# Two graph layers on one core: slot gathers restricted to the chunks that can fill them

## The chip, the cores and the metric

The kernel runs on one core of a Trainium2 chip. The metric is the device time of one launch in microseconds (us). Engines are named as in the profile: PE is TensorE, PEld its weight loads, DVE is VectorE, ACT is ScalarE, POOL is GpSimd, SP is SyncE, which issues DMAs.

## The reference, cut to what matters

Input are 16 graphs of 1024 nodes with 64 channels each, a symmetric 0/1 adjacency of some 1.5%, and a node mask of ones. Layer 0 thins each node's neighbours, adds the node itself, and takes three quantiles of every channel over the neighbours that stay. Layer 1 is three graph convolutions and a linear layer.

```python
h = relu(layernorm(x))
rem = neigh & (sk > 1) & (rank % sk == sk - 1) & mask[:, :, None]
rem = rem | swapaxes(rem, 1, 2)
nd = where(rem, 0.0, adj_) > 0                    # live edges, the node itself included
s = sort(where(nd[..., None], h[:, None], inf), axis=2)
nv = nd.sum(2)                                    # live degree of each node
for tau, w in ((0.25, 0.25), (0.5, 0.5), (0.75, 0.25)):
    pos = tau * (nv - 1)
    agg += w * interpolation of s between floor(pos) and ceil(pos)
x = x + mlp(h + agg)
# layer 1: h = relu(layernorm(x)); three times relu(adj @ (h W)) with a fixed scaling,
# the three results side by side through Wl; x = x + relu(...)
```

## The kernel before

Graphs are worked on in eight pairs, one graph on the lower 64 partitions, one on the upper 64. For each pair there are three kinds of work.

**Preparation** (`prepare`, `prepare_one`, L538 to L782). The adjacency is loaded in eight pieces of 128 rows (L616), made into bytes `edge` (L617) and transposed into `edgeT` (L624, L627). L634 clears the diagonal of both with one multiplication each on DVE. Counts and ranks of neighbours come from matmuls with matrices of ones (`sums`, L664, L669); L690 and its neighbours add up edge, removal and transposed removal in `q`, and L695 leaves the live edges in `edge`, with the live degree `nv`. The nodes of a graph are then put in order of their live degree: `place` (L716) is each node's position, L721 (POOL, indirect DMAs) writes the rows of live edges to DRAM by position, L737 reads them back in order, L747 and L750 transpose them into `liveT`. Its rows are the neighbours in eight chunks of 128, its columns the nodes in order of degree. `nvs` (L760) holds the degrees in that order for both graphs, and `number_slots` (L763, L770 to L776) makes `r`: for each neighbour of a node, the running number of its edge.

**Gather** (L874 to L911). Nodes in order of degree are cut into seven blocks and a tail; `BLOCKS` gives first node, end, least and greatest degree. Slot k of a node is its k-th live neighbour. For every slot DVE fills `s` (L888): a comparison of `r` with the slot's number, over all eight chunks of both graphs. PE multiplies `s` with the channels `hp`, split into three bf16 parts: for each chunk, part and graph one matmul of 64 output rows (L895) adds to `pg`. Several slots share a matmul, up to 400 columns. A node with fewer neighbours than slots gets a large number in every second missing slot (`none`, L905, L908). ACT copies `pg` to `g` (L911). `s` has two buffers, `pg` three.

**Sort** (`quantiles`, L850). A sorting network runs over the slots of a block as minima and maxima on DVE (L858), then the quantiles are summed (L863, L871), and `store` (L918, L920) transposes and sends them off. The second layer (`later`) reads them back with L1098 and runs through L1006, L1010, L1039, L1055 and L1071. The tail's slots of several pairs are kept and sorted together.

Two other parts matter. `layernorm_relu` (L509) ends in a multiplication (L520) and a maximum with zero (L521). `bounds` (L965) runs once in each pair: 16 one-column operations on `nvs` (L971), a maximum over them (L975) and one into `worst` (L976), so that a degree outside `BLOCKS` is noticed. At the end `worst` and `odd` (inputs other than 0 and 1) raise a flag, and a branch then runs `general`, which computes everything again without assumptions.

The main loop interleaves the preparation of the next pair with gather and sort of this one, in steps. Gather of a block is put ahead of the sort of the block before it. The last pair's gather and sort are interleaved with the second layer of all pairs. Within that, the framework orders the instructions of each engine when the kernel is built, so that their order can shift with the change; each engine then runs its list in order.

Of the kernel before, what the change touches and what calls it, by code (L numbers as in the profile page):

```python
# [9 lines left out]
F32 = mybir.dt.float32  # L10
# [11 lines left out]
P = 128  # L22
# [17 lines left out]

TAILS = {4: (0, 4), 7: (4, 7)}
TAIL = (1008, 1024, 21, 42)

SPLIT = 592

# [339 lines left out]
def graph_layers_kernel(ctx: ExitStack, tc: tile.TileContext, ins, out: bass.AP):  # L385
# [54 lines left out]
    wcol = const.tile([P, len(TAUS)], F32, name="wcol")  # L440
    for q, (_, w) in enumerate(TAUS):
        nc.vector.memset(wcol[:, q : q + 1], w)
    worst = const.tile([P, 1], F32, name="worst")
    nc.vector.memset(worst, 0.0)

    odd = const.tile([P, NB, NT], F32, name="odd")

# [61 lines left out]
    def layernorm_relu(pool, h, xt, sq, T):  # L509

        stat = pool.tile([P, T], F32, tag="ln_stat", name="ln_stat")
        nc.vector.tensor_reduce(stat, xt, AX.X, ALU.add)
        nc.vector.tensor_scalar(stat, stat, 1.0 / C, None, ALU.mult)
        nc.vector.tensor_tensor(h, xt, stat[:, :, None].to_broadcast([P, T, C]), ALU.subtract)
        nc.scalar.activation(sq, h, AF.Square)
        var = pool.tile([P, T], F32, tag="ln_var", name="ln_var")
        nc.vector.tensor_reduce(var, sq, AX.X, ALU.add)
        nc.scalar.activation(var, var, AF.Sqrt, bias=eps_ln, scale=1.0 / C)
        nc.vector.reciprocal(var, var)
        nc.vector.tensor_tensor(h, h, var[:, :, None].to_broadcast([P, T, C]), ALU.mult)  # L520
        nc.vector.tensor_scalar(h, h, 0.0, None, ALU.max)  # L521

    h_d = [dram.tile([N, C], F32, name=f"h_d{b}") for b in range(NB)]

# [81 lines left out]
    def prepare_one(st, x, pools):  # L606
# [22 lines left out]
                yield  # L629

        nc.sync.dma_start(out=adjT_d[b][:, :, :], in_=edgeT)
        for e in (edgeT, edge):
            own = diagonal(e)
            nc.vector.tensor_tensor(own, own, other_h[:, None, :].to_broadcast([P, NT, P]), ALU.mult, saturate=False)  # L634
        yield
        sums = chunk_sums(edgeT, pools)
        nbp = ps.tile([P, NT], F32, tag="big", bufs=2, name="nbp")
# [41 lines left out]
        for t in range(NT):  # L679
            q = ps.tile([P, N], F32, tag="big", bufs=2, name="q")  # L680
            for hf in range(NH):
                sl = slice(hf * HALF, (hf + 1) * HALF)
                nc.tensor.matmul(out=q[:, sl], lhsT=ident_h, rhs=edge[:, t, sl], start=True, stop=False)
                nc.tensor.matmul(out=q[:, sl], lhsT=ident_16, rhs=stays[:, t, sl], start=False, stop=False)
                if t // 4 == hf:
                    nc.tensor.matmul(
                        out=q[:, t * P : (t + 1) * P], lhsT=ident_h, rhs=ident_h, start=False, stop=False
                    )
                for u in range(4 * hf, 4 * hf + 4):
                    nc.tensor.matmul(  # L690
                        out=q[:, u * P : (u + 1) * P], lhsT=stays[:, u, t * P : (t + 1) * P], rhs=ident_16,
                        start=False, stop=(u % 4 == 3),
                    )

            nc.scalar.activation(  # L695
                edge[:, t, :], q, AF.Relu, bias=bias(-2.0), accum_out=nv[:, t : t + 1], saturate=False
            )
            yield
# [32 lines left out]
        def find_live():  # L731
# [25 lines left out]
            for hf in range(NH):  # L757
                sl = slice(hf * HALF, (hf + 1) * HALF)
                nc.tensor.matmul(out=nv_all[half, sl], lhsT=all_rows, rhs=sums[:, sl], start=True, stop=True)
            nc.scalar.copy(st.nvs[half, :], nv_all[half, :])  # L760
            yield

            def number_slots(side):  # L763
# [110 lines left out]
    def gather(st, block, g, pools):  # L874


        work, ps, _ = pools
        j0, j1, least, slots = block
        W = j1 - j0
        high = missing_high(slots, least)  # L880
        r, at = (st.r[0], j0) if j1 <= SPLIT else (st.r[1], j0 - SPLIT)
        r = r.rearrange("p x u j -> p (x u) j")
        per = max(1, min(HALF // W, 400 // W))
        for k0 in range(0, slots, per):
            n = min(per, slots - k0)
            s = work.tile([P, n, T2, W], BF16, tag="s", bufs=2, name="s")
            for k in range(n):
                nc.vector.tensor_scalar(  # L888
                    s[:, k], r[:, :, at : at + W], float(LIVE + 1 + k0 + k), None, ALU.is_equal
                )  # L890
            pg = ps.tile([P, n, W], F32, tag="pg", bufs=3, name="pg")
            for u in range(NT):
                for part in range(3):
                    for x in range(2):
                        nc.tensor.matmul(  # L895
                            out=pg[x * C : (x + 1) * C], lhsT=st.hp[:, part, x, u, :], rhs=s[:, :, x * NT + u, :],
                            start=(u == 0 and part == 0), stop=(u == NT - 1 and part == 2),
                        )
                if u:
                    continue  # L900
                for k in range(n):
                    if k0 + k + 1 not in high:
                        continue
                    none = work.tile([P, W], BF16, tag="none", bufs=2, name="none")
                    nc.scalar.activation(none, st.nvs[:, j0:j1], AF.Relu, bias=bias(k0 + k + 0.5), scale=-1.0)  # L905
                    for x in range(2):
                        half = slice(x * C, (x + 1) * C)
                        nc.tensor.matmul(  # L908
                            out=pg[half, k], lhsT=ident_big[:, half], rhs=none, start=False, stop=False
                        )  # L910
            nc.scalar.copy(g[:, k0 : k0 + n, :], pg)  # L911

# [39 lines left out]
    def sort_tails(first, end, pools):  # L952
# [8 lines left out]
        quantiles(work, TAIL, (g, t), tail_z[:, :, first:end].rearrange("p q p2 w -> p q (p2 w)"), agg)  # L961
        for p in range(first, end):
            store(p, agg, slice((p - first) * TW, (p - first + 1) * TW), TAIL[0], pools)

    def bounds(st, pools):  # L965

        work = pools[0]
        out_by = work.tile([P, 2 * len(BLOCKS) + 2], F32, tag="out_by", name="out_by")
        for i, (j0, j1, least, most) in enumerate(BLOCKS + (TAIL,)):
            for k, (j, sign, edge) in enumerate(((j0, -1.0, least), (j1 - 1, 1.0, -most))):  # L970
                nc.vector.tensor_scalar(  # L971
                    out_by[:, 2 * i + k : 2 * i + k + 1], st.nvs[:, j : j + 1], sign, float(edge), ALU.mult, ALU.add
                )
        most_by = work.tile([P, 1], F32, tag="most_by", name="most_by")
        nc.vector.tensor_reduce(most_by, out_by, AX.X, ALU.max)  # L975
        nc.vector.tensor_tensor(worst, worst, most_by, ALU.max)  # L976


    def channels_first(pools, src, tag):
# [295 lines left out]
    with ExitStack() as stack:  # L1275
# [7 lines left out]
        with ExitStack() as inner:  # L1283
            early = (
                inner.enter_context(tc.tile_pool(name="early", bufs=1)), keep,
                inner.enter_context(tc.tile_pool(name="ps_early", bufs=1, space=PSUM)),
            )

            ahead = Steps(prepare(0, early))
            ahead.rest()  # L1290
            st = ahead.result
            gather_block(st, 0, pools)
            for p in range(NP - 1):
                ahead = Steps(prepare(p + 1, early))
                for n in range(last + 1):
                    for _ in range(11):
                        ahead.step()
                    if n == 0 and p in TAILS:

                        sort_block(st, n, pools)  # L1300
                        gather_block(st, n + 1, pools)
                        sort_tails(*TAILS[p], pools)
                        continue
                    if n < last:
                        gather_block(st, n + 1, pools)
                    else:
                        ahead.rest()
                        gather_block(ahead.result, 0, pools)
                    sort_block(st, n, pools)
                bounds(st, pools)  # L1310
                st = ahead.result


        with ExitStack() as inner:
# [5 lines left out]
            for n in range(last + 1):  # L1320
# [8 lines left out]
                if n < last:  # L1329
                    gather_block(st, n + 1, pools)  # L1330
                sort_block(st, n, pools)
            bounds(st, pools)
            done.sent = NP
            ahead.rest()

# [1 line left out]
    with ExitStack() as stack:  # L1337
        ps = stack.enter_context(tc.tile_pool(name="ps_flag", bufs=1, space=PSUM))
        most_odd = const.tile([P, 1], F32, name="most_odd")
        nc.vector.tensor_reduce(most_odd, odd.rearrange("p b t -> p (b t)"), AX.X, ALU.max)  # L1340
        nc.vector.tensor_tensor(worst, worst, most_odd, ALU.max)
        pd = ps.tile([1, P], F32, name="pd")
        nc.tensor.transpose(pd, worst, ident)
        most = const.tile([1, 1], F32, name="most")
        nc.vector.tensor_reduce(most, pd, AX.X, ALU.max)
        nc.vector.tensor_scalar(most, most, 0.0, None, ALU.is_gt)
        flag = const.tile([1, 1], I32, name="flag")
        nc.vector.tensor_copy(flag, most)
# [28 lines left out]
```

## Time and profile before

| | |
|---|---|
| median of 3 runs | 3311.39 us (3309.24 to 3313.25) |
| the profiled execution | 3304.46 us, of which span 3302.7 us |
| mean granted PE clock | 0.917 |
| busy: PE / DVE / ACT / POOL | 83% / 81% / 51% / 13% of the span |
| matmuls of gather (L895) | 18432, PE busy with them 1525.3 us |
| fills of `s` (L888) | 1312, DVE busy with them 684.4 us |
| minima and maxima (L858), three largest groups | 319.8, 288.3 and 209.6 us |

An engine's busy time is the union of its instructions' times, so that overlapping instructions are not counted twice. In a group's row stand the operation with its shapes, the count, the busy time, the mean duration in ns, and after the second bar the idle time before its instructions with what ended it.

### The profile page before, as it was taken

What the parts mean: (1) busy time and instruction counts of PE and PEld (TensorE: products, weight loads), DVE (VectorE), ACT (ScalarE), POOL (GpSimd) and SP (SyncE); (2) the same over time, 40 slices, a digit from 0 to 9 for tenths busy, and PEclk for the clock granted to TensorE, in tenths of its full rate; (3) what the DMA queues carried; (4) which work ended last, traced back from release to release, by engine and by line L of the source; (5) the groups of instructions that cost most, each with busy time, mean ns of one, the idle gap of its engine ahead of it and who ended that gap; (6) DMA issues with size and microseconds to landing.
All of it is one profiled execution on the core that took longest, in us unless ns stands there. A gap on an engine that the chain in (4) does not pass through costs nothing. (4 is left out here: it accounts for less than half of the span.)

```text
span 3302.7 us, 69626 instructions
## 1 busy us (share of the span) xinstructions
PE 2727.0 (83%) x29049; PEld 1787.7 (54%) x29049; DVE 2672.2 (81%) x6053; ACT 1691.7 (51%) x3260; POOL 439.7 (13%) x416
## 2 busy tenths in 40 slices
PE   3679978987898789878697898789977689888878
PEld 2446645664566456545464566456644357655545
DVE  4158999899989998898999989898996887874332
ACT  4776547655765566556454765475552323232222
POOL 0211020121012001200101012101103120221110
PEclk9789989998999899989898999799988799989989
DMA  4131113101311130114001310131103110212211
GB/s 132 50 105 59 31 46 105 48 23 37 114 39 34 36 110 33 38 39 119 32 20 42 106 47 23 37 108 45 36 16 69 11 47 11 52 47 59 51 52 40
DMA packets 220069, 177.58 MB, mean 54 GB/s; under 512 B 188001, under 2 KB 188129, under 8 KB 215649
## 3 DMA queue, kind: packets, MB, share of 16 engines
q1 hardware_dynamic: 141824, 125.88, 12.6%
q0 software_dynamic: 16384, 37.77, 3.7%
q10 hardware_dynamic: 61536, 9.39, 1.9%
q8 instruction: 229, 3.75, 0.5%
q14 instruction: 96, 0.78, 0.1%
HBM read 124.44 MB, written 48.55 MB: 52 GB/s over the span
## 5 line engine op out<-in xcount | busy, mean ns | idle before, releaser
L895 PE MATMUL pg<-s,hp 128*64 128x400 bf16 (+5 forms) x18432 | 1525.3, 317 | 92.0 <-DVE s L888 71.9
L895 PEld LDWEIGHTS <-hp 128*64 128x64 bf16 x18432 | 997.6, 112 | 512.5 <-issue 96.6
L888 DVE TENSOR_SCALAR s<-r 128x256 bf16<-128x256 bf16 (+6 forms) x1312 | 684.4, 571 | 122.0 <-PE pg L895 107.9
L911 ACT COPY g<-pg 128x400 f32<-128x400 f32 (+10 forms) x384 | 169.1, 441 | 507.2 <-PE pg L895 445.1
L721 POOL DMA_INDIRECT live_d<-edge,place x128 | 194.3, 1518 | 1061.5 <-DVE place L716 1027.4
L1055 PE MATMUL pg<-adjT,xw 128*64 128x512 fp8e4 x2304 | 294.0, 403 | 44.0 <-issue 22.3
L858 DVE TENSOR_TENSOR t<-g 128x600 f32<-128x600 f32 (+9 forms) x524 | 319.8, 631 | 10.9 <-ACT g L911 9.0
L858 DVE TENSOR_TENSOR g<-t 128x96 f32<-128x96 f32 (+16 forms) x555 | 288.3, 541 | 1.5
L793 ACT ACTIVATE coef<-z,bias 128x200 f32<-128x200 f32 (+6 forms) x480 | 174.3, 402 | 169.1 <-DVE agg L871 153.3
L1055 PEld LDWEIGHTS <-xw 128*64 128x64 bf16 x2304 | 140.7, 115 | 178.9 <-issue 68.4
L1098 POOL DMA_INDIRECT agg<-agg_d,place x128 | 141.9, 1108 | 560.9 <-PE pt L986 312.1
L858 DVE TENSOR_TENSOR t<-t 128x192 f32<-128x192 f32 (+20 forms) x447 | 209.6, 481 | 0.5
L737 POOL DMA_DIRECT2D lp<-live_d x128 | 83.0, 649 | 808.6 <-PE pt L747 772.2
L796 ACT ACTIVATE coef<-coef,wcol 128x200 f32<-128x200 f32 (+7 forms) x512 | 188.9, 399 | 1.8 <-issue 0.7
L619 DVE SCALAR_TENSOR_TENSOR junk_v<-a 128x1024 fp8e4<-128x1024 f32 x128 | 156.4, 1222 | 40.4 <-DMA a<-in_adj 39.2
L750 ACT ACTIVATE liveT<-pt 128x1024 fp8e4<-128x1024 f32 x128 | 129.3, 1024 | 89.7 <-PE pt L747 89.6
L617 ACT ACTIVATE edge<-a 128x1024 fp8e4<-128x1024 f32 x128 | 134.5, 1057 | 62.6 <-DMA a<-in_adj 62.1
L747 PE MATMUL pt<-ident_h,lp 128*128 128x128 bf16 x1024 | 98.8, 254 | 81.0 <-ACT liveT L750 43.5
L713 ACT ACTIVATE junk<-keys,minus 128x1024 fp8e4<-128x1024 f32 x128 | 144.3, 1128 | 38.5 <-PE keys L706 37.4
L776 ACT CAST r<-pr 128x592 bf16<-128x592 f32 (+1 forms) x256 | 141.7, 586 | 42.1 <-PE pr L772 40.9
L695 ACT ACTIVATE edge<-q,bias 128x1024 fp8e4<-128x1024 f32 x128 | 141.9, 1110 | 41.4 <-PE q L690 32.2
L673 ACT ACTIVATE stays<-cs,back 128x1024 f16<-128x1024 f32 x128 | 136.4, 1116 | 35.8 <-DVE look L654 21.4
(172 smaller groups left out, 3768.9 us busy)
## 6 DMA issues: line engine op xcount, KB each, us to landing
a<-in_adj SPq DMA_DIRECT2D x128, 512.0 KB
adjT_d<-edgeT SPq DMA_DIRECT2D x16, 1024.0 KB
lp<-live_d POOLq DMA_DIRECT2D x128, 128.0 KB
adjT<-adjT_d SPq DMA_DIRECT2D x16, 1024.0 KB
room<-in_x SPq DMA_DIRECT2D x16, 256.0 KB
h_d<-room SPq DMA_DIRECT2D x16, 256.0 KB
h_again<-h_d SPq DMA_DIRECT2D x16, 256.0 KB
xt<-in_x SPq DMA_DIRECT2D x16, 256.0 KB
```

Source lines behind the costliest of these rows:

```text
L619: nc.vector.scalar_tensor_tensor(junk, a, 1.0, a, ALU.is_equal, ALU.not_equal, accum_out=odd[:, b, t : t + 1], saturate=False)
L695: nc.scalar.activation(edge[:, t, :], q, AF.Relu, bias=bias(-2.0), accum_out=nv[:, t : t + 1], saturate=False)
L713: nc.scalar.activation(junk, keys, AF.Sign, bias=minus[:, t : t + 1], accum_out=above[:, t : t + 1], saturate=False)
L721: sent = nc.gpsimd.indirect_dma_start(out=live_d[b][:, :], out_offset=bass.IndirectOffsetOnAxis(ap=place[:, b, t : t + 1], axis=0), in_=ed ...
L793: nc.scalar.activation(coef[:, i, :], z[:, at], AF.Abs, bias=bias(rank - (slots + 1) // 2 + tau), scale=sign)
L796: nc.scalar.activation(coef[:, i, :], coef[:, i, :], AF.Relu, bias=wcol[:, q : q + 1], scale=-w)
L858: nc.vector.tensor_tensor(view(bufs, o, n1, n2), view(bufs, a, n1, n2), view(bufs, b, n1, n2), ALU.max if op else ALU.min)
L888: nc.vector.tensor_scalar(s[:, k], r[:, :, at : at + W], float(LIVE + 1 + k0 + k), None, ALU.is_equal)
L895: nc.tensor.matmul(out=pg[x * C : (x + 1) * C], lhsT=st.hp[:, part, x, u, :], rhs=s[:, :, x * NT + u, :], start=(u == 0 and part == 0), st ...
L911: nc.scalar.copy(g[:, k0 : k0 + n, :], pg)
L1055: nc.tensor.matmul(out=pg[cs, :], lhsT=part[:, u, cs], rhs=adjT[x][:, u, sl], start=(u == 0 and k == 0), stop=(u == NT - 1 and k == len(xw ...
L1098: nc.gpsimd.indirect_dma_start(out=agg[:, t, x, :], out_offset=None, in_=agg_d[b][:, :], in_offset=bass.IndirectOffsetOnAxis(ap=place[:, b ...
```

## The change

Neighbours come in ascending order, in eight chunks of 128. Slot k of a node can lie in chunk c only if the node has at most k live neighbours ahead of the chunk and more than k up to its end. A new table `NEAR` gives, for each block: the greatest number of neighbours up to the end of a chunk (`first`), the least number (`end`), and, for high slots, how many nodes at the start of the block are known to have no such slot (`fewer`). Gather takes from it the chunks of every slot and the first column `w0`; fills and matmuls cover these alone. Where no chunk is looked into by all slots of a group, two matmuls with a block of zeros start the sum instead.

The table is checked: for each graph, matmuls of `chunk_to` with `sums` make the number of neighbours up to each chunk, an identity matmul adds `bounds`, and ACT sums what is above zero into `beyond`. This takes the place of the old `bounds` function. The rows of `bounds` are made on POOL at the start, by 97 memsets and 32 small DMAs. Further, the diagonal of `edge` is no longer cleared on DVE: in `q`, the diagonal block is taken from `edgeT` instead. And layernorm's last two operations become one.

```diff
+    bounds = const.tile([C, HALF], BF16, name="bounds")
+    beyond = const.tile([2 * NT, NB], F32, name="beyond")
...
+            for row, pieces in ((c - 1, most), (NT + c - 1, least)):
+                line = setup.tile([1, N], BF16, tag="line", name="line")
+                for value, a, b in pieces:
+                    nc.gpsimd.memset(line[:, a:b], value)
+                for hf in range(NH):
+                    nc.gpsimd.dma_start(
+                        out=bounds[32 * hf + row : 32 * hf + row + 1, :], in_=line[:, hf * HALF : (hf + 1) * HALF]
+                    )
...
-        nc.vector.tensor_tensor(h, h, var[:, :, None].to_broadcast([P, T, C]), ALU.mult)
-        nc.vector.tensor_scalar(h, h, 0.0, None, ALU.max)
+        nc.vector.scalar_tensor_tensor(h, h, 0.0, var[:, :, None].to_broadcast([P, T, C]), ALU.max, ALU.mult)
...
-        for e in (edgeT, edge):
-            own = diagonal(e)
-            nc.vector.tensor_tensor(own, own, other_h[:, None, :].to_broadcast([P, NT, P]), ALU.mult, saturate=False)
+        own = diagonal(edgeT)
+        nc.vector.tensor_tensor(own, own, other_h[:, None, :].to_broadcast([P, NT, P]), ALU.mult, saturate=False)
...
-                nc.tensor.matmul(out=q[:, sl], lhsT=ident_h, rhs=edge[:, t, sl], start=True, stop=False)
+                others = [sl]
                 if t // 4 == hf:
+                    others = [slice(sl.start, own.start), slice(own.stop, sl.stop)]
+                    nc.tensor.matmul(out=q[:, own], lhsT=edgeT[:, t, own], rhs=ident_h, start=False, stop=False)
+                    nc.tensor.matmul(out=q[:, own], lhsT=ident_h, rhs=ident_h, start=False, stop=False)
+                for o in others:
+                    if o.start < o.stop:
+                        nc.tensor.matmul(out=q[:, o], lhsT=ident_h, rhs=edge[:, t, o], start=False, stop=False)
...
+            by = ps.tile([2 * NT, N], F32, tag="big", bufs=2, name="by")
+            for hf in range(NH):
+                sl = slice(hf * HALF, (hf + 1) * HALF)
+                rows = slice(32 * hf, 32 * hf + 2 * NT)
+                nc.tensor.matmul(out=by[:, sl], lhsT=chunk_to, rhs=sums[:, sl], start=True, stop=False)
+                nc.tensor.matmul(
+                    out=by[:, sl], lhsT=ident_h[rows, rows], rhs=bounds[rows, :], start=False, stop=True
+                )
+            junk = work.tile([P, N], F8, tag="junk", name="junk")
+            nc.scalar.activation(
+                junk[: 2 * NT, :], by, AF.Relu, accum_out=beyond[:, b : b + 1], saturate=False
+            )
...
-                    s[:, k], r[:, :, at : at + W], float(LIVE + 1 + k0 + k), None, ALU.is_equal
+                    s[:, k, :, us, w0:], r[:, :, us, at + w0 : at + W], float(LIVE + 1 + k0 + k), None, ALU.is_equal
...
+            looks = [(u, [k for k in range(n) if u in chunks[k]]) for u in range(NT)]
+            looks = sorted((look for look in looks if look[1]), key=lambda look: -len(look[1]))
+            whole = len(looks[0][1]) == n and not w0
+            if not whole:
+                for x in range(2):
+                    nc.tensor.matmul(
+                        out=pg[x * C : (x + 1) * C].rearrange("p k w -> p (k w)"), lhsT=ident_h[C:, :C],
+                        rhs=st.hp[C:].rearrange("p a x t c -> p (a x t c)")[:, : n * W], start=True, stop=False,
+                    )
...
-                            out=pg[x * C : (x + 1) * C], lhsT=st.hp[:, part, x, u, :], rhs=s[:, :, x * NT + u, :],
+                            out=pg[x * C : (x + 1) * C, ks, w0:], lhsT=st.hp[:, part, x, u, :],
+                            rhs=s[:, ks, x, u, w0:], start=(whole and i == 0 and part == 0),
...
-    def bounds(st, pools):
```

Of the chunks of each slot in the block of nodes 592 to 768, for example, the table leaves: slots 0 and 1 chunks 0 to 5, slots 2 and 3 chunks 0 to 6, slots 4 to 12 all eight, slots 13 and 14 chunks 1 to 7, slots 15 and 16 chunks 2 to 7, and slot 16 without the block's first 48 nodes.

## The prediction

> **What bounds the kernel now.** I read the page's busy table and slices first, then the busy time by stage, then the waits of the long middle stage, then the groups of instructions kept apart by shape.
>
> ```profile
> PE 2727.0 (83%) x29049; PEld 1787.7 (54%) x29049; DVE 2672.2 (81%) x6053; ACT 1691.7 (51%) x3260; POOL 439.7 (13%) x416
> ...
> PE   3679978987898789878697898789977689888878
> ...
> DVE  4158999899989998898999989898996887874332
> ...
> PEclk9789989998999899989898999799988799989989
> ```
>
> (The three digit rows are forty equal slices of 82.6 us.) Over the span VectorE and TensorE look alike. By stage they don't:
>
> ```profile
> core 0: us, PE busy (x) PEld busy (x) DVE busy (x) ACT busy (x) POOL busy (x), PEclk, DMA share, GB/s
> 0.00:200.00 200.00, 98.71 (x793) 63.83 (x794) 58.01 (x195) 120.51 (x158) 28.80 (x42) 0.83 0.30 89
> 200.00:2500.00 2300.00, 1959.57 (x22517) 1296.72 (x22516) 2114.43 (x4669) 1360.42 (x2639) 286.72 (x262) 0.93 0.18 56
> 2500.00:2990.00 490.00, 410.96 (x3763) 266.92 (x3763) 394.82 (x1044) 137.49 (x346) 77.71 (x66) 0.87 0.17 33
> 2990.00:3302.70 312.70, 257.74 (x1979) 160.20 (x1977) 104.92 (x148) 73.31 (x118) 46.50 (x48) 0.92 0.19 51
> ```
>
> The first 200 us prepare pair 0 alone; no engine is full. From 200 to 2500 us the pairs overlap: DVE is busy 2114 of 2300 us (92%), PE 85%. From 2500 to 2990 us the last pair is sorted beside the second layer. The last 313 us are the second layer alone, a chain through PE.
>
> ```profile
> PE pt_agg L918 <- DVE agg L871: 93.7, 26, 9.4
> ...
> DVE s L888 <- PE pg L895: 89.4, 48, 5.7
> ...
> PE pg L895 <- DVE s L888: 65.8, 55, 11.1
> ```
>
> These are waits inside 200 to 2500 us: total us, times, longest. PE stands idle for DVE 159 us (first and third line), DVE for PE 89 us. So the middle is set by DVE, with PE close behind; ACT, at 59%, sets nothing.
>
> **What the Trainium skill says.** "VectorE: DVE Perf Modes", section "What auto-detection actually checks": a one-source operation runs in the fourfold mode if its tensors are 16-bit with unit step and the outermost non-unit dimensions are even or equal. The fill of `s` agrees: 221 ns for 256 elements and 989 ns for 3200 give (989-221)/2944 = 0.261 ns per element. "TensorE: Matmul & The Clock Gate", section "Wait, 56ns, not 53.3ns?": back-to-back matmuls start every N/2.4 GHz plus 2.5 ns. In the trace the two column halves start together, and such couples of 352 columns follow each other at 149 ns, couples of 96 at 43 ns: price and width go together, down to the smallest. "TensorEngine Tiling", "Key Properties": a change of tiling mode drains the engine. In the trace a 128x128 matmul of 128 columns is followed after 56 ns by one of its kind and after 149 ns by a 128x64 one, so 93 ns. "GPSIMD Engine Reference", "1. Specifications": POOL shares its SBUF interfaces with VectorE. The copies of L930 take 197 ns at best and 1127 ns in the median, so yes.
>
> **The change, part by part.** First the fills and the matmuls of gather. I ran its two loops over the tables by hand.
>
> ```profile
> L888 DVE TENSOR_SCALAR s<-r 128x3200 bf16<-128x3200 bf16 x208 | 199.4, 989 | 39.8 <-PE pg L895 27.7 <-issue 10.8 <-ACT r L776 1.3
> L888 DVE TENSOR_SCALAR s<-r 128x256 bf16<-128x256 bf16 x336 | 51.3, 221 | 0.0
> L634 DVE TENSOR_TENSOR edge<-edge,other_h 128x1024 fp8e4<-128x1024 fp8e4 x16 | 19.6, 1224 | 20.6 <-PE ptE L624 20.5
> L971 DVE TENSOR_SCALAR out_by<-nvs 128x1 f32<-128x1 f32 x128 | 9.8, 144 | 0.0
> ```
>
> DVE: the 1312 fills stay 1312, but their elements per partition go from 2,099,200 to 1,858,432. The 240,768 fewer at 0.261 ns are **62.8 us**. 824 of the fills become partial; their outermost dimension is the two graphs, which is even, so I take the fourfold mode for all. The clearing of `edge` goes: **19.6 us**. The bounds operations go: 9.8 us, and eight reductions of 170 ns and eight maxima of 160 ns: **12.5 us**. The layernorm's product (1.22 us, L520) and maximum (0.69 us, L521) become one three-operand instruction, priced by the row of L1078 at 1.22 us: 16 x 0.69 = **11.0 us**, half of it in the second layer. Seventeen small memsets and two operations at the end add 1.5 us. DVE sum: 62.8 + 19.6 + 12.5 + 11.0 - 1.5 = **104.4 us less**.
>
> PE: gather's matmuls go from 18,432 to 16,976, and their columns from 6,297,600 to 5,598,592, the new seeding matmuls included. In couples that is 349,504 columns / 2.4 GHz + 728 x 2.5 ns = 147.4 us less. Against it: `by`, four matmuls of 512 columns (216 ns each) for each of 16 graphs, 13.8 us; the 64 seeded groups, whose 64-row operand I take as a mode of its own, two changes of 93 ns, 11.9 us (nothing if it is no change of mode); the split of L683, 192 more matmuls with no more columns, 0.5 us. Sum: **121 us less** at full clock, 132 us at the mean of 0.917.
>
> ACT: 16 activations on `by` at 1.11 us plus 0.19 us for the accumulator (row of L695): 21 us more, spread over 16 graphs, on an engine at 59%. `by` takes one of the two `big` buffers for about 2 us; behind it stand the numbering matmuls (L770). While gather matmuls of the pair before fill PE, that is covered. In pair 0 nothing covers it: 2 x (0.9 to 1.7 + 1.3), so 4 to 6 us, against 2.4 us of clearing, 0.7 us of layernorm and 1.5 us of bounds operations gone there. I book zero for the first 200 us, with ends of -4 and +6.
>
> POOL: 97 memsets and 32 DMA issues before its first scatter (L721), which waits for `place` and starts at 110 us. The small DMAs of L737 take 536 to 650 ns: 32 x 0.65 = 21 us. Memsets: 100 ns for one element and 204 ns for 128 (the rows at the start) make 0.82 ns an element, so 0.94 us for the 16 full lines, 15 us, and some 13 us for the 81 short ones; hand-overs between them add 6 us. That is 55 us. If every busy microsecond of DVE in the first 100 us (39) held POOL up as at L930, 94 us: still ahead of 110. Cost zero; at worst some 20 us at the front. The DMAs are 64-byte pieces on queues with 0.36 of their time in use.
>
> **On the path.** In 200 to 2500 us lie 7/8 of fills, clearing, bounds and prepare's layernorms: 54.9 + 17.2 + 10.9 + 4.8 = 87.8 us, counted in full since DVE sets that stage. From 2500 to 2990 us: 7.9 + 1.6 us and two layernorms, 11 us. In the last chain a few layernorms, 1.5 us. Sum 100 us. PE drops by 6% of its share, DVE by 4%, so DVE's 89 us of waits for `pg` should shrink also; I add 5 us. From the profiled execution's 3304.5 us this makes 3199.5; the median of the runs is 6.9 us above that execution, so **3206 us**, within 3190 to 3222 if this case holds.
>
> **The rivals.**
> - PE sets more than I think: the waits for `pg` and the windows in which PE is 95% busy and DVE 90% (900 to 1000 us) speak for it, the 159 us of PE waiting against it. Then the gain is PE's, 121 to 145 us: about 3175. Chance 0.12.
> - A wait takes the place of half the gain. `s` has two buffers; a fill that is done earlier waits for matmuls that still use the other. Also the order on DVE shifts: most instructions keep their places, but sort and fill are interleaved differently. For it: 48 waits of that kind now. Against it: the matmuls shrink by a larger share than the fills. About 3258. Chance 0.14.
> - Slower: the partial fills lose the fourfold mode. Their 764,800 elements cost 0.26 ns more each in the twofold mode, 199 us, against 104 us saved: 3311 + 95 = 3406; in the onefold mode 3800. It decides as soon as more than half of these elements fall to the twofold mode. Against it: the source of the full fills is strided too and runs fourfold. Chance 0.05.
> - The change doesn't do what it says: a table that is too tight raises the flag, and the general path recomputes all 16 graphs, far beyond any range here. Counted from the inputs, the prefix counts touch the tables and nowhere exceed them. Chance 0.01.
>
> **How the numbers follow.** The forecast has 0.68. The range 3162 to 3262 reaches over the first two rivals and leaves out the last two. About 0.2%, 7 us, is what a measurement here tells from no change. Faster: 0.68 + 0.12 + most of 0.14 = 0.93; within: 0.01; slower: 0.06.
>
> **What would show it.** Right: partial fills lie on the line 154 ns + 0.261 ns per element; DVE busy near 2568 us, PE near 2600; DVE still about 92% busy in the middle; POOL's setup done by 95 us and the first scatter near 110. Wrong: a fill of 2000 elements above 0.8 us; DVE below 90% in the middle with longer waits for `pg`; the first scatter late; a later start of the last stage not explained by these.

## The result and the profile after

The changed kernel takes 3227.23 us (median of 4, 3222.94 to 3232.01) against 3310.31 us (median of 4, 3308.27 to 3313.25): ratio 0.9749, 95% interval 0.9732 to 0.9766, 83 us less. Run again on another chip, its ratio was 0.9792 (0.9778 to 0.9805). The two intervals don't meet, so ratios from different chips are good to about 0.4%, 14 us; where less matters, I compare kernels of one chip. The profiled execution took 3232.01 us, the slowest of its four, with a span of 3230.2 us; so the profiled executions differ by 72 us only.

The busy table and three of its slice rows, of the kernel after:

```profile
PE 2602.9 (81%) x27819; PEld 1728.7 (54%) x27849; DVE 2569.1 (80%) x5895; ACT 1714.2 (53%) x3292; POOL 461.8 (14%) x545
...
PE   3689968987898689867686799689976689898878
...
DVE  4149999899889988998997889988996888793332
...
PEclk9779989998999799988797799889988799899999
```

VectorE (DVE) lost 103.1 us of work, TensorE (PE) 124.1, ScalarE gained 22.5. These are nearly the sums of the forecast (104.4, 121 to 132, 21). What is new is in the eighteenth to twenty-third slice (1370 to 1860 us): PE stands at 6, 7, 6, 8, 6, 7 tenths there, before at 7, 8, 6, 9, 7, 8. By stage, after (columns as in the forecast's table):

```profile
0.00:200.00 200.00, 101.69 (x815) 65.42 (x818) 55.21 (x201) 121.69 (x160) 67.23 (x172) 0.82 0.29 89
200.00:2500.00 2300.00, 1900.59 (x21740) 1271.88 (x21767) 2061.06 (x4554) 1392.93 (x2690) 272.69 (x261) 0.91 0.19 56
2500.00:2990.00 490.00, 405.63 (x3714) 265.55 (x3713) 373.27 (x1030) 144.10 (x353) 91.31 (x80) 0.89 0.17 40
2990.00:3230.20 240.20, 195.02 (x1555) 125.86 (x1554) 79.58 (x111) 55.43 (x90) 30.61 (x32) 0.92 0.18 49
```

DVE is busy 2061 of 2300 us in the middle, 89.6%, where it was 92%, though each window now holds more of the program. The longest waits of DVE and PE in the same stretch, after (total us, times, longest):

```profile
DVE s L962 <- PE pg L993: 135.3, 64, 21.3
...
PE pt_agg L1005 <- DVE agg L933: 91.1, 19, 11.3
...
PE pg L993 <- DVE s L962: 66.3, 33, 11.7
PE pt L796 <- DMA lp<-live_d: 62.7, 18, 22.4
```

The fills' wait for `pg` did not shrink; it rose from 89.4 to 135.3 us, with one wait of 21.3 us. DVE below 90% in the middle with longer waits for `pg` is one of the signs of being wrong that the forecast names. PE has one of 22.4 us, for a DMA.

Fixed windows drift against the program, so I cut both traces at the first fill of each pair. The last pair runs to the last sum of quantiles, the rest follows (lengths in us, profiled executions):

| kernel | start | pairs 0 to 3 | pair 4 | pairs 5, 6 | last pair | rest |
|---|---|---|---|---|---|---|
| before | 202.2 | 312.8, 317.4, 320.1, 320.6 | 362.5 | 321.0, 313.4 | 512.6 | 320.0 |
| after | 205.4 | 304.7, 307.2, 308.7, 309.3 | 381.2 | 311.7, 304.2 | 480.3 | 317.6 |
| difference | +3.2 | -8.1, -10.2, -11.4, -11.3 | **+18.7** | -9.3, -9.2 | **-32.3** | -2.4 |

The six ordinary pairs gained 59.5 us, the last pair 32.3. Pair 4, in which the collected tails are sorted too, lost 18.7.

### What happened in pair 4

POOL in pair 4, after: start, length, instruction, and in brackets the idle time before it. These are the first three of graph 11's eight scatters:

```profile
1684.62 4.10 POOL L770 DMA_INDIRECT live_d<-edge,place  x1 [8.30 <-DVE place L765]
1689.02 14.40 POOL L770 DMA_INDIRECT live_d<-edge,place  x1 [0.30 <-issue]
1703.73 1.22 POOL L770 DMA_INDIRECT live_d<-edge,place  x1 [0.30 <-issue]
```

The same two first scatters in the kernel before:

```profile
1728.71 1.16 POOL L721 DMA_INDIRECT live_d<-edge,place  x1 [7.48 <-DVE place L716]
1730.18 1.03 POOL L721 DMA_INDIRECT live_d<-edge,place  x1 [0.31 <-issue]
```

The second scatter held POOL for 14.40 us instead of about one. PE after, in the same stretch:

```profile
1690.99 1.07 PE L796 MATMUL pt<-ident_h,lp 128*128 128x128 bf16 x16
1714.41 1.89 PE L796 MATMUL pt<-ident_h,lp 128*128 128x128 bf16 x16 [22.35 <-DMA lp<-live_d]
```

In PE's list the transposes of graph 11's rows stood next, their rows were not in DRAM, and the gather matmuls behind them waited too; with them DVE's fills for a free `s`, one of them for 21.3 us. From the first scatter's start to the last one's end the eight took 27.4 us, before 11.2. The kernel before has long scatters elsewhere: the first one of graphs 3, 5, 7, 9 and 13 took 7.62 or 7.63 us each. None of these is left after the change, so that the 128 scatters' total time even fell, from 194.3 to 175.4 us.

### The profile page after: what moved, and what is told of

Read it like the earlier page. It is cut to its first block, busy times and chain, and to the rows that moved or that the text cites. A ratio compares the mean times of both kernels' runs of the same rounds, so it can differ in the third digit from the quotient of the medians.

```text
span 3230.2 us, 67236 instructions
## 1 busy us (share of the span) xinstructions
PE 2602.9 (81%) x27819; PEld 1728.7 (54%) x27849; DVE 2569.1 (80%) x5895; ACT 1714.2 (53%) x3292; POOL 461.8 (14%) x545
## 5 line engine op out<-in xcount | busy, mean ns | idle before, releaser
L993 PE MATMUL pg<-s,hp 128*64 128x400 bf16 (+11 forms) x16848 | 1361.8, 314 | 93.2 <-DVE s L962 92.7
L993 PEld LDWEIGHTS <-hp 128*64 128x64 bf16 x16848 | 907.4, 113 | 452.1 <-issue 75.3
L962 DVE TENSOR_SCALAR s<-r 128x3200 bf16<-128x3200 bf16 (+25 forms) x1312 | 621.1, 520 | 144.2 <-PE pg L993 143.9
L920 DVE TENSOR_TENSOR t<-g 128x600 f32<-128x600 f32 (+9 forms) x524 | 319.8, 628 | 12.9 <-ACT g L998 11.1
L770 POOL DMA_INDIRECT live_d<-edge,place x128 | 175.4, 1371 | 1025.3 <-DVE place L765 870.9
L1129 PE MATMUL pg<-adjT,xw 128*64 128x512 fp8e4 x2304 | 285.5, 400 | 39.6 <-DVE xw L1119 28.9
L920 DVE TENSOR_TENSOR g<-t 128x96 f32<-128x96 f32 (+16 forms) x555 | 285.8, 539 | 1.4
L920 DVE TENSOR_TENSOR t<-t 128x192 f32<-128x192 f32 (+20 forms) x447 | 208.5, 478 | 0.4
L832 PE MATMUL pr<-liveT,upto 128*128 128x512 fp8e4 (+2 forms) x384 | 124.7, 343 | 50.3 <-ACT r L838 41.3
L796 PEld LDWEIGHTS <-lp 128*128 128x128 fp8e4 x1024 | 82.9, 117 | 145.0 <-DMA lp<-live_d 101.0
L762 ACT ACTIVATE junk<-keys,minus 128x1024 fp8e4<-128x1024 f32 x128 | 144.4, 1128 | 29.8 <-PE keys L755 28.7
```

The lines of the kernel that those rows point to most:

```text
L762: nc.scalar.activation(junk, keys, AF.Sign, bias=minus[:, t : t + 1], accum_out=above[:, t : t + 1], saturate=False)
L770: sent = nc.gpsimd.indirect_dma_start(out=live_d[b][:, :], out_offset=bass.IndirectOffsetOnAxis(ap=place[:, b, t : t + 1], axis=0), in_=ed ...
L796: nc.tensor.matmul(out=pt[:, u, :], lhsT=lp[:, u * P : (u + 1) * P], rhs=ident_h, start=True, stop=True)
L920: nc.vector.tensor_tensor(view(bufs, o, n1, n2), view(bufs, a, n1, n2), view(bufs, b, n1, n2), ALU.max if op else ALU.min)
L962: nc.vector.tensor_scalar(s[:, k, :, us, w0:], r[:, :, us, at + w0 : at + W], float(LIVE + 1 + k0 + k), None, ALU.is_equal)
L993: nc.tensor.matmul(out=pg[x * C : (x + 1) * C, ks, w0:], lhsT=st.hp[:, part, x, u, :], rhs=s[:, ks, x, u, w0:], start=(whole and i == 0 an ...
```

## The experiments

Ratios are to the kernel before on the same chip. The first four ran on one chip, the next four on a second, the last four on a third. On the third, the changed kernel took 3249.41 us and the kernel before 3319.29.

| kernel | ratio | 95% interval |
|---|---|---|
| e1_full_fills | 0.9836 | 0.9820 to 0.9852 |
| e2_full_matmuls | 0.9887 | 0.9869 to 0.9905 |
| e3_rest_only | 1.0054 | 1.0037 to 1.0071 |
| e4_short_pause | 0.9719 | 0.9698 to 0.9740 |
| e5_gather_only | 0.9803 | 0.9778 to 0.9828 |
| e6_no_check | 0.9674 | 0.9647 to 0.9701 |
| e7_no_step | 0.9766 | 0.9742 to 0.9791 |
| e8_relief_only | 0.9950 | 0.9931 to 0.9969 |
| e9_after_again | 0.9792 | 0.9778 to 0.9805 |
| e10_double_check | 0.9730 | 0.9712 to 0.9748 |
| e11_one_mode | 0.9678 | 0.9662 to 0.9693 |
| e12_one_mode_pause | 0.9626 | 0.9613 to 0.9640 |

### Which engine sets the gain: fills or matmuls

e1 leaves the fills at all chunks and columns:

```diff
-  s[:, k, :, us, w0:], r[:, :, us, at + w0 : at + W]
+  s[:, k], r[:, :, :, at : at + W]
```

e2 brings the matmuls back to their old number and width in the groups that are not seeded: in place of a chunk that only some slots look into, the matmuls of a chunk that all look into are issued once more, so that the sums are not the right ones. The seeded groups stay narrow:

```diff
+  if whole:
+      most = looks[0]
+      looks = [look if len(look[1]) == n else most for look in looks] + [most] * (NT - len(looks))
```

e3 empties the table, so that both are full, and keeps the rest of the change:

```diff
-  first, end, fewer = NEAR[(BLOCKS + (TAIL,)).index(block)]
+  first, end, fewer = {}, {}, {}
```

e1: 

> The changed kernel, with the fills of s over all chunks and columns as before (DVE busy with them 684 us again, 63 more than in the changed kernel) and the matmuls still restricted. Theory (DVE sets the middle, PE the last stage): seven pairs lose most of 7.85 us each, some 45 us, the last stage little: about 3272 us; with another order around the fifth pair 3250 to 3290. Rival (PE sets the pace throughout): no loss, 3222 to 3235.

e2: 

> The changed kernel, with restricted fills, and with full-width matmuls in all groups that aren't seeded: for a chunk that only some slots look into, the matmuls of a chunk that all look into are issued once more (so the sums, and the output, are not the reference's). PE gets 513,408 columns back, 107 us at full clock; DVE's work is that of the changed kernel. Theory (DVE sets the middle, PE the last stage): the last stage loses about 15 us, the middle up to 20: 3242 to 3262. Rival (PE sets the pace throughout): 3335 to 3350.

e3: 

> The changed kernel with an empty table for gather: fills and matmuls in full, but the diagonal of edge not cleared, the bounds operations gone, layernorm's fused operation, and by with its check in place (POOL's setup too). DVE has 41 us less than before, PE 14 us more, ACT 21 us more. Theory (DVE sets the middle): 3272 to 3290. Rival (PE or ACT sets the pace): 3310 to 3325.

On the same chip e3 takes 3324.33 us, e1 3250.28, e2 3267.83, and e4, which has both restrictions and a pause that is told of below, 3211.60. None of the four has the scatter of 14.40 us (the longest of graph 11 are 7.61, 2.61, 7.11 and 4.16 us), so nothing has to be taken off for the pause. The narrow matmuls alone (e1) bring 74 us, both together (e4) 113; so the narrow fills bring 39 where the matmuls are narrow already. e2 brings 56, but not by its fills alone: its gather matmuls keep PE busy for 1482.9 us, against 1516.8 in e3 and 1361.3 in e4, so that it keeps about a fifth of PE's saving. Whether the two reliefs add up is therefore not shown.

If DVE alone set the middle, e1 would have gained nothing there; its six ordinary pairs take 1867.0 us against 1915.6 in e3. If PE alone set it, e4 would have gained nothing over e1; its six take 1847.6. **Neither engine sets the middle alone.** The expectations for e1 and e2, in which DVE set it, missed: e1 came to 3250 us, not to some 3272, and e2 to 3268, above its 3262.

The last pair is different. It took 506.8 us in e3, 507.7 in e2 with its narrow fills, 481.4 with narrow matmuls alone. There PE sets the time.

Last, e3 is slower than the kernel before, by 18 us, though by the forecast's sums DVE has 41 us less to do (30.6 between the two traces). Its time lies in the range of the rival, but not for the rival's reason, as e8 will show: something in the rest of the change costs more than 18 us.

### What the check costs

e5 is the kernel before with the restricted fills and matmuls alone: no `by`, no rows of `bounds`, the other operations of DVE as before. Its edit is the gather part of the diff above. e6 is the kernel after without the check and its setup on POOL:

```diff
-            by = ps.tile([2 * NT, N], F32, tag="big", bufs=2, name="by")
...
-                junk[: 2 * NT, :], by, AF.Relu, accum_out=beyond[:, b : b + 1], saturate=False
-            )
-            yield
+    nc.vector.memset(beyond, 0.0)
```

e7 is the kernel after without the check's own step, that is, without the `yield` behind `junk`:

```diff
                 junk[: 2 * NT, :], by, AF.Relu, accum_out=beyond[:, b : b + 1], saturate=False
             )
-            yield
```

e8 is e6 with the emptied table of e3.

e5: 

> The kernel before with the restricted gather alone: the table, fills, matmuls and seeds of the changed kernel; both diagonals cleared on DVE, the old bounds operations, layernorm in two operations, and nothing that verifies the table. Against before: DVE 63 us less, PE 135 us less. Theory now (in the middle both engines bind together, each worth about half of what it is relieved of, and the remaining parts of the change gain nothing): 3195 to 3225, no slower than the changed kernel. Rival (DVE sets the middle, as forecast, so that 41 us of DVE's work put back are lost in full): 3255 to 3270.

e6: 

> The changed kernel without the verification of the table (by, bounds, their setup on POOL, and the step of the preparation that by makes); the output stays the reference's. PE has 14 us less than in the changed kernel, ACT 21 us. Theory (the check is on the path by half of its PE time, and its extra step moves the preparation against the gather): 3195 to 3215. Rival (it is covered, as forecast): 3222 to 3232.

e7: 

> The changed kernel with by in place, but without the step of its own that it makes in the preparation (the yield after it is dropped), so that the interleaving of preparation and gather is counted as before. Theory (the moved steps cost, not the operations): 3200 to 3215. Rival (the operations themselves cost, or nothing does): 3222 to 3235.

e8: 

> The kernel before with DVE relieved of 41 us (diagonal of edge, bounds operations, fused layernorm), gather in full, and nothing that verifies a table. PE and ACT have the work of before. Theory (both engines bind together, so that a relief of DVE alone is taken up by PE): 3285 to 3306. Rival (DVE sets the middle, as forecast): 3262 to 3275.

From the medians, against 3324.95 us for the kernel before on this chip: relief of DVE alone 16 us (e8, 3308.82), restricted gather alone 67 (e5, 3257.88), both 106 (e6, 3218.69), both and the check without its step 79 (e7, 3245.91). So the check costs 27 us, where the forecast had zero; and e7's ratio lies between the two of the full change, so the step has no part in it that these runs show: the theory for e7 fell.

e5 fell too, into its rival's range. The same relief of DVE, 41 us by the forecast's sums, brings 16 us beside the full gather (e8) and 39 beside the restricted one (e6 against e5). What a relief of one engine is worth depends on how much the other has to do. Where the 39 us lie is open: in the profiled executions, the fastest of e5 and the slowest of e6, the seven pairs take 2211.6 and 2211.1 us, and e6 is shorter only behind them.

My next theory was that PE's time for the check lies on the path. PE in the changed kernel, at the change into pair 2 (e9, the changed kernel once more):

```profile
801.10 0.38 PE L815 MATMUL by<-sums,chunk_to 128*16 128x512 bf16 x1
801.41 0.38 PE L816 MATMUL by<-bounds,ident_h 16*16 16x512 bf16 x1
801.72 0.38 PE L815 MATMUL by<-sums,chunk_to 128*16 128x512 bf16 x1
802.03 0.38 PE L816 MATMUL by<-bounds,ident_h 16*16 16x512 bf16 x1
```

The four start 0.31 us apart. In e11, told of next, all four have operands of 128 rows, and they start 0.215 us apart:

```profile
763.89 0.38 PE L810 MATMUL by<-sums,chunk_to 128*16 128x512 bf16 x1
764.10 0.38 PE L811 MATMUL by<-bounds,ident_h 128*16 128x512 bf16 x1
```

So each change between operands of 128 and of 16 rows costs some 0.093 us. With as much on entry, an estimate is 1.33 us a graph, 21 us in all, against 13.8 in the forecast. e10 issues the whole block, from `by` to `junk`, a second time behind the first. e11 gives all of `by`'s operands 128 rows, puts `by` ahead of `nv_all`, and has no step for it:

```diff
-    bounds = const.tile([C, HALF], BF16, name="bounds")
+    bounds = const.tile([P, HALF], BF16, name="bounds")
+    nc.vector.memset(bounds, 0.0)
...
-                    out=by[:, sl], lhsT=ident_h[rows, rows], rhs=bounds[rows, :], start=False, stop=True
+                    out=by[:, sl], lhsT=ident_h[:, rows], rhs=bounds, start=False, stop=True
...
-            yield
```

e9: 

> The changed kernel once more, so that the three beside it have it on their chip: about 0.974 of the kernel before. The fifth pair of graphs again some 375 to 382 us, with TensorE standing still behind graph 11's scatters.

e10: 

> The changed kernel with the block that makes the tile by (its four matmuls and the junk reading) issued a second time right behind the first, for every graph; the sum that it leaves in beyond is the same. Theory: the check's TensorE time lies on the path, about 21 us of it for 16 graphs and the wait for junk's reading beside it, so a second copy costs 20 to 30 us: ratio 0.981 to 0.984. Rival, the forecast's own step (the check lies beside other work): no more than 0.3% over the changed kernel, 0.974 to 0.977.

e11: 

> The changed kernel with every matmul of the tile by taking 128-row operands (bounds made 128 rows, zero below and between, and the whole columns of ident_h), with by placed ahead of nv_all, and without by's own step. Theory: the mode changes inside by, about 93 ns for each of four matmuls plus one on entry, 7 to 8 us over 16 graphs, are part of what the check costs, so the ratio falls by 0.2 to 0.4%: 0.970 to 0.972. Rival (they lie beside VectorE's work): the same as the changed kernel within 0.2%.

**The theory fell.** The doubled check puts off the numbering matmuls behind it by another 2.6 us in the first graph of a pair and 1.4 in the second, 31 us in all, and yet e10 is 0.6% faster than e9. Part of this lead is another thing: e10 happens not to have the scatter of 14.40 us. The same scatter in e10:

```profile
1688.86 2.95 POOL L770 DMA_INDIRECT live_d<-edge,place  x1 [0.30 <-issue]
```

Its pair 4 took 366.3 us, that of e9 377.5. But in the six ordinary pairs, too, nothing is lost by the second copy (1838.5 us against 1846.2), and e4, which also is without the long scatter, has a ratio of 0.9719 against 0.9730. e11 keeps the whole check and saves at most 8 us of mode changes; it has the long scatter as e9 has, and yet it is 1.2% (39 us) faster, where 0.2 to 0.4% were expected, and at 0.9678 as fast as the kernel without the check (0.9674, on another chip). What PE, ScalarE and `big` spend on the check is hidden, as forecast; what the check costs comes in another way.

Cutting the traces at the fills shows where. For the seven changes from one pair to the next, in us added up:

| kernel | last fill to the next pair's first | first fill to the thirteenth | sum |
|---|---|---|---|
| before | 123.3 | 277.6 | 400.9 |
| e8 (no check, full gather) | 124.1 | 280.8 | 404.9 |
| e5 (no check) | 112.5 | 275.7 | 388.2 |
| e6 (no check) | 108.5 | 277.6 | 386.1 |
| e11, e12 (by first) | 114.2, 112.1 | 269.9, 268.1 | 384.1, 380.2 |
| after, e9 | 180.9, 177.2 | 231.5, 231.0 | 412.4, 408.2 |
| e10 (twice) | 177.0 | 236.0 | 413.0 |
| e7 (no own step) | 175.8 | 231.8 | 407.6 |
| e3 (full gather) | 181.3 | 241.0 | 422.3 |

There are two kinds and nothing between (e1, e2 and e4 have 173 to 180 us in the first column). With the check behind `nv_all`, some 25 us pass at each change before the next pair's first fill; without it, or with `by` ahead of `nv_all`, 15 to 18. Most of it comes back in the fills after it, and 17 to 33 us over seven changes don't: 21.5 between e7 and e6, 24.0 between e9 and e11. DVE at the change into pair 2, in e9 (start, length, instruction):

```profile
810.36 1.22 DVE L622 TENSOR_TENSOR h_again<-h_again,hp 128x1024 f32<-128x1024 f32 x1
...
813.18 1.22 DVE L624 TENSOR_TENSOR hp<-h_again,hp 128x1024 bf16<-128x1024 f32 x1
...
818.23 0.98 DVE L962 TENSOR_SCALAR s<-r 128x3200 bf16<-128x3200 bf16 x1
```

and in e11:

```profile
803.37 0.98 DVE L961 TENSOR_SCALAR s<-r 128x3200 bf16<-128x3200 bf16 x1
804.28 1.22 DVE L623 TENSOR_TENSOR h_again<-h_again,hp 128x1024 f32<-128x1024 f32 x1
```

In e9 the first fill stands behind the preparation of `hp` and more of the sorting (L920). No wait is marked on it, and what it reads had been there for 8.2 us, as the last copy of the first columns of `r` by ScalarE shows:

```profile
809.37 1.08 ACT L838 CAST r<-pr 128x592 bf16<-128x592 f32 x2
```

At all seven changes of e9 it had been there for 7.4 to 8.3 us, and in e10, where the second check makes it come later, still for 5.4 to 6.7: so the check's own time is swallowed here. The fill simply comes later in DVE's list. Between the last fill and the first stand 89 or 90 DVE instructions in every kernel of the one kind (after, e1 to e4, e7, e9, e10), and 51 or 52 in every kernel of the other. From the operation on `nvs` (L611, at 802.12 us) it is 16.1 us to the fill; in e11 the same operation starts at 796.33, 7.0 us before it. PE over the whole change, from the last fill to the first, e9 and then e11 (busy times in the order of the stage table):

```profile
793.00:818.20 25.20, 18.98 (x149) 10.12 (x147) 24.23 (x98) 20.78 (x47) 2.46 (x3) 0.87 0.17 57
```

```profile
786.20:803.40 17.20, 13.81 (x128) 8.43 (x126) 15.28 (x61) 13.53 (x35) 2.45 (x3) 0.85 0.10 36
```

DVE is busy all through both, but PE idles 6.2 us in the first and 3.4 in the second. Gather's first matmul follows the last fill after 30 us in e9 and 28 in e11 (212.6 and 197.2 us over seven changes). Of the 616 DVE instructions between two pairs' first fills, 77 stand elsewhere in e11 than in e9, 8 between e11 and e6, none between e9 and the first run of the changed kernel. So the check's price goes with the **other order that the framework makes** of DVE's list when this block stands where it stands. That the order is the cause, and not only goes with it, was not put to a run of its own: no kernel has the check where it stands and the old order by force. Whether e11's place for `by` or its one mode turned the order back was not separated either; dropping the step alone (e7) did not.

### The scatter of graph 11

```diff
+        own_place = place[:, b, :]
+        if b == 11:
+            own_place = work.tile([P, 2], I32, tag="own_place", name="own_place")
+            nc.vector.tensor_copy(own_place, place[:, b, :2])
...
+            at = own_place if t < 2 else place[:, b, :]
...
+            if b == 11 and t == 1:
+                nc.vector.memset(own_place, 0)
```

The memset waits until two scatters have read their copy of the places, and DVE pauses so long. (The edit gives the copy to the first two scatters; the trace writes its name to the second and third.)

e4: 

> The changed kernel; for graph 11 alone the first two scatters of POOL take their places from a small copy, which DVE then overwrites, so that DVE stops there until these two scatters are done. In the changed kernel they take 4.1 and 14.4 us beside an unbroken run of DVE operations, and PE then stands still for 22 us. Theory (POOL is held up by DVE, and this costs the fifth pair what it lost): both scatters take under 2 us each, PE's wait is below 10 us, the fifth pair takes 355 to 365 us in place of 381, and the time is 3202 to 3215. Rival (the long scatter is not DVE's doing, or the fifth pair is long for another reason): the scatter stays long, or the pair stays at 375 to 385 us and the time at 3222 to 3232.

POOL in e4:

```profile
1682.02 4.16 POOL L775 DMA_INDIRECT live_d<-edge,place  x1 [8.55 <-DVE g L927]
1686.49 0.99 POOL L775 DMA_INDIRECT live_d<-edge,own_place  x1 [0.30 <-issue]
```

and DVE in e4:

```profile
1690.32 0.06 DVE L785 MEMSET own_place<- 128x2 int32 x1 [5.01 <-DMA live_d<-edge,own_place]
```

A pause of 5.01 us brings the second scatter from 14.40 to 0.99 us, the group from 27.4 to 13.6, DVE's wait for `pg` in this pair from 29.8 to 8.3, and pair 4 from 381.2 to 366.5 (377.5 and 375.9 in e9 and e7, which have the scatter of 14.40 us too). The first scatter, which began before the pause, still took 4.16 us, more than the 2 expected. A pause is not the only thing that does it: e1 and e10 have no scatter of pair 4's graph 11 above 3 us without one, and e1 has more work for DVE. So it depends on what DVE does at that moment, and a change elsewhere in the kernel can bring or remove it.

The version that the runs point to, e11 and this pause together:

e12: 

> The kernel of one mode, with a pause of VectorE for the first two scatters of graph 11 besides (they read a copy of their places, and a memset of that copy waits for them). Theory: the gains add up, 7 to 12 us for the modes and 12 to 16 us for the pause: ratio 0.966 to 0.969, below the changed kernel and the kernel with the pause alone (0.972). Rival: the pause only, 0.970 to 0.972.

Here the gain over e11 on the same chip is 15 us, and e12 beats both kernels: 3195.67 us against 3249.41 for the changed one and 3319.29 before. Both gains add up, to somewhat more than expected, and the rival of the pause alone is out, since e12 lies 1.7% below e9. In the profiled executions pair 4 takes 372.8 us in e11 and 368.7 in e12; PE's longest wait for the rows, 22.3 us in e11, is gone, but the pair gains 4 us only. So a pause is worth 4 to 15 us of pair 4 in the traces and 15 us in these medians.

## Why the prediction was right, and where its steps were not

The forecast was 3206 us, 105 less; it came to 3227, 83 less, inside the range and outside the 3190 to 3222 of its own case. The sums of work held. The way from them to the time did not, and that the time came so near is in part luck: an error in the seven pairs and an opposite one in the last pair met.

**The sums of work.** DVE 104.4 us less was forecast, 103.1 came. PE 121 to 132, 124.1 came. ScalarE 21 more, 22.5 came. Two terms of PE were small by 7 and 2 us: `by` (21 for 13.8, its own mode changes were not counted) and the seeds (13.8 for 11.9; entering the mode costs 98 ns, leaving it 117).

**The fills** keep the fourfold mode, as the Trainium skill's "VectorE: DVE Perf Modes" (What auto-detection actually checks) led to expect. Three shapes of the kernel after, the middle and last only partly looked into:

```profile
L962 DVE TENSOR_SCALAR s<-r 128x3200 bf16<-128x3200 bf16 x136 | 130.3, 988 | 10.3 <-PE pg L993 10.2
L962 DVE TENSOR_SCALAR s<-r 128x1440 bf16<-128x1440 bf16 x48 | 22.8, 526 | 2.4 <-PE pg L993 2.4
L962 DVE TENSOR_SCALAR s<-r 128x64 bf16<-128x64 bf16 x32 | 3.4, 167 | 0.0
```

154 + 0.261 x 1440 is 530, measured 526; for 64 elements 171, measured 167. The rival that ends slower is out by this.

**The start.** Zero was booked, with ends of -4 and +6; it took 3.2 us more. POOL's setup was far from late:

```profile
108.39 1.04 POOL L770 DMA_INDIRECT live_d<-edge,place  x1 [62.33 <-DVE place L765]
```

POOL had stood idle for 62 us when graph 0's places came: done by 46 us, where 55 to 94 was the estimate.

**"87.8 us, counted in full since DVE sets that stage", and 5 us of shorter waits.** This is the step that failed. The seven pairs gained 40.8 us, not 92.8. Two terms were missing. One goes with the order of DVE's list at seven changes of pair, some 21 to 24 us (e7 to e6, e9 to e11): I had costed `by` by its engine time and its buffer, and named the shifting order only within a rival, beside the two buffers of `s`. The other is graph 11's scatters, some 15 us (e12 to e11; e4: 381.2 to 366.5): I had looked for POOL behind DVE in the setup, at the start, and not at the scatters in mid-run, although the Trainium skill's page that I cited for it, "GPSIMD Engine Reference", 1. Specifications (POOL shares its SBUF interfaces with VectorE), is not about the start alone. The trace agrees in e4: 14.40 us became 0.99 with DVE paused. In e12, which has neither, the seven pairs take 2183.6 us on its chip, against 2267.9 for the kernel before on the first: 84 less. But e11, with the long scatter, takes 2186.3, in the fastest of its five executions, while e12's traced one is the slowest of its five; so one execution each does not split the 84 between the two. The reason behind "in full" was wrong all the same: e1 gains without the fills' relief.

The forecast left out a third thing: the mean granted PE clock, which it took from before (0.917), was 0.902 after. PE ran at half clock for 632 us of the span, before for 547. An estimate from these two is that PE lost at most 43 us of work by it, half of the 85 us more. Whether any of this came into the time, no run shows; e6, at 0.897 in its traced execution, is faster all the same.

**"From 2500 to 2990 us, 11 us".** The last pair gained 32.3. It was priced by DVE, but PE sets it (e1 and e2).

**The last chain**, 1.5 us forecast, gained 2.4.

**The rivals.** "A wait takes the place of half the gain" came nearest in kind (waits for `pg` rose to 135.3 us, 21.3 of it behind the scatter); whether the two buffers of `s` have a part in the rest, no run tells. "PE sets more" is true of the last pair and half true of the middle. The errors that met in the sum are 52 us too much in the seven pairs and 21 too little in the last one. Even e6, without the check and 106 us faster, is no proof of the 105: it still has the long scatter in pair 4 (26.8 us for its group).

## What to carry over

Where a framework orders each engine's list, an added block can cost, beside its engine time, whatever order it brings: look in the traces at the changes between stages, at what stands ahead of the first instruction that feeds the other engine, and try the block in a second place before paying for it. Two engines at 85% and 92% of the same stage, as here, can bind it together: relief of either gained, and what it gained changed with the load of the other, so relieve both, and price each stage by its own bound. One late DMA held up PE's whole list for 22 us here, so look also at the issuing engine's longest single instruction. And before two kernels are compared as a test of one thing, see in their traces whether another, such as this scatter, differs between them too.

## What the runs showed of the hardware that was not expected

- An indirect scatter that takes POOL 0.96 us at best held it 14.40 us in the middle of a dense run of DVE work, in two runs of the changed kernel on two chips to the same 0.01 us; with 5 us of pause for DVE it took 0.99. In the kernel before, five others took 7.62 or 7.63 us. Which of DVE's operations hold it is open: after the pause the next scatters took 0.96 to 1.24 us with DVE busy again.
- PE ran at half clock for 632 us of the span after and 547 before, although it had less to do; in pair 4 alone 129.5 us against 75.1. What lowered it was not looked into.
- Matmuls whose operands alternate between 128 and 16 rows start 0.31 us apart, with 128 rows throughout 0.215: some 93 ns for each change, as much as a change between 128x128 and 128x64.
